# Normed rows turned into columns by the DMA crossbar instead of TensorE, with norm factors folded into weights and a new piece order, in a two-layer graph kernel

## The chip, the cores and the metric

The kernel runs on one core of one Trainium2 chip. The time is the device time of one execution in microseconds (us); the kernel before was run three times. A profile is one separate execution recorded by the hardware profiler; its span runs from the first to the last instruction.

The engines are named as in the profile: PE is TensorE's matmul stream and PEld its weight loads, DVE is VectorE, ACT is ScalarE, POOL is GpSimd, SP is SyncE, which issues most DMAs here. L459 is line 459 of the kernel before.

## The reference, cut to what matters

64 graphs of 256 nodes with 256 features each go through two layers. Every graph is independent of the others; all share the weights.

```python
# layer 0, per graph: x [256,256], adj [256,256] of 0 and 1
h = gat(x, adj, W1, a1); h = gat(h, adj, W2, a2)     # att = softmax(where(adj>0, leaky_relu(e), NEG)); att @ (h W)
h = layernorm(x + h) * g_ln1 + b_ln1                                  # norm A
x = layernorm(h + relu(h @ w_ff1 + b_ff1) @ w_ff2 + b_ff2) * g_ln2 + b_ln2   # norm B
# layer 1: 8 heads of 32
q, k = x @ Wq + bq, x @ Wk + bk
attn = softmax(q k^T / sqrt(32))
out = sum over r in 0..3 of (attn * (adj == r)) @ (x @ Wv[r] + bv[r])
y = layernorm(x + out @ Wo + bo) * g1 + beta1                         # norm C
out = layernorm(y + gelu(y @ W1 + b1) @ W2 + b2) * g2 + beta2         # norm D
```

## The kernel before, in words

**Tiling.** A graph's 256 rows are two tiles of 128 partitions. Everything is fp32. Products with weights want the features on the partitions ("columns"), norms want the nodes there ("rows"), so after norms A, B and C the normed rows are turned into columns: `to_columns` (L355) issues four TensorE transposes of 128x128 into a PSUM bank (L362), and two ACT instructions (L369) copy them out, with the norm's g as scale and its b as bias. The rows are also needed as a residual: `scaled` (L339) multiplies them by g and adds b on POOL (L344, L351). The feed-forward products and the values use seven products in place of eight (`seven_products`, L393), for which `combine` (L378) forms four sums of the columns on POOL (L389).

**Heads.** The scores (L636) go through a maximum on DVE (L643), exponentials on ACT (L650), division by the sums on POOL (L662), and then each of the eight heads' 256x256 weights are turned by the DMA crossbar: `turned` (L272) views the fp32 words as 2-byte halves, lets one DMA transpose turn them (L282, piece `dt`), sorts the halves by four DMAs of 64 KB in pieces of 256 bytes (L290, piece `dm`), and one copy of 128x1024 2-byte values on ACT or POOL joins the halves into fp32 words (L300, piece `mg`). By DVE these are multiplied with the adjacency (L669), and TensorE forms the outputs (L677).

**Order.** The work of a graph is cut into some 170 pieces. Each belongs to one of five stages: L (loads), G (graph attention and norm A), F (feed-forward, norm B, queries and keys), A (attention), T (the rest). The list `PERIOD` (L44) is the order, written out, in which the pieces of one period are issued; in a period graph b is in stage L, graph b-1 in G, b-2 in F, b-3 in A, b-4 in T. The loop at L747 runs 67 periods. Every engine takes its own instructions strictly in this order, so a piece that waits holds up all later pieces of its engine; SP is such a queue too, and carries nearly all DMAs. PSUM has eight banks of one tag "mm", and a matmul piece needs a free one. The tiles of `turned` ("pairs", "halves") have two buffers each.

A piece is named by stage, step and key: `G.gB` is the second graph attention's product (L562), `G.lnA`, `G.rsA`, `G.nmA` are norm A's sums (DVE), root (POOL) and scaling (DVE, L331); `F.ha` to `F.he` are the seven products (L459), `F.hk1` and so on their copies (L438, ACT) and additions (L441, DVE), `F.r0` to `F.r3` the activations (L473, ACT; `T.ge0` to `T.ge3` in layer 1), `F.f0`, `F.f1` the second feed-forward product (L481), `F.q`, `F.k` the queries and keys (L597), `A.sc0`, `A.sc1` scores, `A.va` to `A.ve` values (L610), `A.o0`, `A.o1` outputs (L677), `T.wo` their projection (L696), `T.out` the store.

Weights that are not needed at once are loaded in the first periods (`after`, L257). Ahead of the loop, `joint_weights` (L186) forms W1 W2. After it, a check at L66 to L84 finds whether the adjacency held anything but 0 and 1, in which case a general version would run; here it does not.

Of the kernel before, what the change touches and what calls it, by code (L numbers as in the profile page):

```python
# [25 lines left out]
F32 = mybir.dt.float32  # L26
U8 = mybir.dt.uint8
U16 = mybir.dt.uint16
I32 = mybir.dt.int32
# [4 lines left out]
P = 128  # L34
# [7 lines left out]
STAGES = "LGFAT"  # L42

PERIOD = """  # L44
A.sc0 A.mx02 A.mx00 T.wo A.ex02 G.wh0 A.mx03 A.rz02 A.ex00 A.mx01 A.rz00 T.lnC F.tA A.sp02 G.wc0
F.cA0 F.cA1 A.sp00 A.dt02 A.sc1 A.dt00 G.wh1 A.ex01 F.ha A.mx10 F.sA A.ex03 T.rsC F.hb G.wc1 F.raA
A.ex10 A.mx12 F.hk1 F.hk2 G.eA A.rz01 A.mx13 T.nmC A.dm02 G.lrA T.tC A.ex12 A.rz10 T.cC0 F.hc
A.sp10 G.away A.rz03 T.cC1 F.hp1 A.ex13 A.dm00 A.sp01 A.va G.adA F.hk3 A.mg02 A.rz12 A.vk1 A.dt10
T.ha L.xT A.rz13 A.vb F.hp3 T.hk1 F.hd T.sC T.raC A.mg00 A.vk2 G.exA T.hb A.vc F.hp2 G.rzA A.vp1
T.hk2 F.r0 F.r1 A.mx11 A.vk3 A.dt01 F.he F.hk4 F.rbA F.r2 T.hc G.gA0 A.vd G.gA1 A.dm10 A.vp3 T.hk3  # L50
A.sp03 A.sp13 F.r3 A.mg10 A.ex11 A.dm01 A.dt03 T.hd T.hp3 T.hp2 T.hp1 A.pm02 A.pm10 A.pm00 G.wd0
A.rz11 A.sp11 T.ge0 A.dt13 A.mg01 F.f0 A.vp2 T.ge1 T.he F.f1 T.hk4 G.wd1 T.ge2 T.ge3 T.rbC G.eB
A.sp12 A.pm01 F.lnB G.lrB A.dm03 A.dm13 G.adB A.dt11 A.mg03 F.rsB F.nmB F.raB A.ve T.f0 A.pm03
T.f1 A.mg13 A.dt12 A.dm11 G.exB A.pm13 G.rzB F.tB F.cB0 F.cB1 F.sB G.gB T.lnD A.mg11 A.vk4 G.lnA
A.dm12 L.x F.q T.rsD F.k A.mg12 G.rsA A.o0 F.qe0 F.qe1 A.pm11 A.pm12 T.nmD T.raD F.ke0 T.rbD A.o1
F.ke1 A.oc0 L.adj G.nmA T.out F.rbB A.oc1
# [3 lines left out]
@with_exitstack  # L60
def gnn_stack(ctx: ExitStack, tc: tile.TileContext, t, out: bass.AP):
    nc = tc.nc
    keep = ctx.enter_context(tc.tile_pool(name="keep", bufs=1))

    ends = keep.tile([P, 2, t["x"].shape[0]], F32, name="ends")
    binary(tc, t, ends, out)  # L66
    with ExitStack() as last:
        psum = last.enter_context(
            tc.tile_pool(name="lpsum", bufs=1, space=bass.MemoryType.PSUM)
        )  # L70
        beyond = keep.tile([P, 3], F32, name="beyond")
        nc.vector.memset(beyond, 1.0)
        nc.vector.tensor_scalar(ends[:, 0, :], ends[:, 0, :], 1.0, 1.0, ALU.is_gt, ALU.mult)
        nc.vector.tensor_scalar(ends[:, 1, :], ends[:, 1, :], 0.0, 1.0, ALU.is_lt, ALU.mult)
        nc.vector.tensor_reduce(beyond[:, :2], ends, AX.X, ALU.max)
        total = psum.tile([1, 2], F32, name="total")
        nc.tensor.matmul(total, beyond[:, 2:3], beyond[:, :2], start=True, stop=True)
        found = keep.tile([1, 2], F32, name="found")
        nc.vector.tensor_copy(found, total)
        others = keep.tile([1, 1], I32, name="others")  # L80
        nc.vector.tensor_tensor(others, found[:, 0:1], found[:, 1:2], ALU.max)
    any_other = nc.values_load(others, min_val=0, max_val=P)
    with tc.If(any_other > 0):
        general(tc, t, out)  # L84
# [3 lines left out]
def binary(ctx: ExitStack, tc: tile.TileContext, t, ends, out: bass.AP):  # L88
# [38 lines left out]
    joined = work.tile([P, 4, D], F32, tag="v", name="joined", bufs=1)  # L127
# [17 lines left out]
    def half_factors(name, width, block):  # L145
# [7 lines left out]
        def differences(*before):  # L153
            for to, a, b in (*before, (3, 5, 0), (4, 2, 3), (5, 2, 5), (6, 1, 4)):
                nc.gpsimd.tensor_tensor(f[:, to, :], f[:, a, :], f[:, b, :], ALU.subtract)

        return f, differences

# [5 lines left out]
    def load(do, b):  # L164
# [7 lines left out]
        def adjacency():  # L172
            adj = tiles["adj"] = io.tile([P, NT * N], I32, tag="adj", name=f"adj_{b}", bufs=3)
# [56 lines left out]
    rows = {n: row(t[n], n) for n in ("L0_gnn_g_ln1", "L0_gnn_b_ln1", "L0_gnn_b_ff2")}  # L230
    differences()
    norms.append((column("L0_gnn_g_ln2"), column("L0_gnn_b_ln2")))
    wk, wq = (weight(f"L1_gnn_{n}", KC) for n in ("Wk", "Wq"))
    bk, bq = column("L1_gnn_bk"), column("L1_gnn_bq")
    nc.gpsimd.tensor_scalar(bq, bq, QSCALE, 1.0, ALU.mult, ALU.mult)
# [7 lines left out]
    late = {}  # L243

# [12 lines left out]
    def after(period):  # L257

        if period == 1:
            value_differences((5, 5, 0), (2, 2, 1))  # L260
            late_weights()
            join_biases(("bv1", "bv0", ALU.subtract))
            join_biases(("L0_gnn_b_ln1", "L0_gnn_b_ff2"), ("L0_gnn_b_ln2", "L1_gnn_bo"))
        elif period == 2:
            late["differences"]()
# [6 lines left out]
    def turned(do, stage, key, name, src, tile_of, keep, engine):  # L272
# [5 lines left out]
        def turn():  # L278
            t["pairs"] = work.tile([P, 4, 2, P], U16, tag="pairs", name=f"pairs_{name}", bufs=2)
            words = src()  # L280
            flat = words.rearrange("p a b n -> p (a b n)") if len(words.shape) == 4 else words
            nc.sync.dma_start_transpose(  # L282
                out=t["pairs"].rearrange("p k c q -> p (k c) q"), in_=flat.bitcast(U16)
            )

        def part():
            t["halves"] = work.tile([P, 2, 4, P], U16, tag="halves", name=f"halves_{name}", bufs=2)
            for s in range(2):
                for c in range(2):
                    nc.sync.dma_start(  # L290
                        out=t["halves"][c * 64 : (c + 1) * 64, s, :, :],
                        in_=t["pairs"][s::2, :, c, :],
                    )

        def join():
            to = tile_of()
            keep(to)
            flat = to[:, 0, :]
            copy = nc.scalar.copy if engine == "ACT" else nc.gpsimd.tensor_copy
            copy(  # L300
                flat.bitcast(U16).rearrange("p (n s) -> p s n", s=2),
# [3 lines left out]
        do[f"{stage}.dt{key}"], do[f"{stage}.dm{key}"], do[f"{stage}.mg{key}"] = turn, part, join  # L305


    def layernorm(do, stage, key, name, src):
# [19 lines left out]
        def norm():  # L328
            y = tiles["y"] = work.tile([P, KC, NT, P], F32, tag="y", name=f"y_{name}", bufs=3)
            for i in range(NT):  # L330
                nc.vector.tensor_scalar(  # L331
                    y[:, :, i, :], tiles["acc"][:, i, :].rearrange("p (c d) -> p c d", c=KC),
# [6 lines left out]
    def scaled(do, stage, key, name, tiles, g, b):  # L339


        def times():
            tiles["res"] = work.tile([P, NT, D], F32, tag="res", name=f"res_{name}", bufs=3)
            nc.gpsimd.tensor_tensor(  # L344
                tiles["res"].rearrange("p t (c d) -> p t c d", c=KC),
                tiles["y"].rearrange("p c t d -> p t c d"),
                over_nodes(g).rearrange("p t (c d) -> p t c d", c=KC), ALU.mult,
            )
# [6 lines left out]
    def to_columns(do, stage, key, name, tiles, g, b):  # L355


        def turn():
            ps = tiles["t"] = mm_tile(f"t_{name}")
            for c in range(KC):  # L360
                for i in range(NT):
                    nc.tensor.transpose(  # L362
                        ps[:, c, nodes(i)], tiles["y"][:, c, i, :], ident
                    )

        def scale(c):
            if c == 0:
                tiles["cols"] = work.tile([P, KC, N], F32, tag="cols", name=f"cols_{name}", bufs=3)
            nc.scalar.activation(  # L369
                tiles["cols"][:, c, :], tiles["t"][:, c, :], AF.Identity,  # L370
                bias=b[:, c : c + 1], scale=g[:, c : c + 1],
            )

        do[f"{stage}.t{key}"] = turn
        for c in range(KC):
            do[f"{stage}.c{key}{c}"] = partial(scale, c)
# [116 lines left out]
    def gat(do, b, tiles):  # L493
# [4 lines left out]
        def away():  # L498
# [4 lines left out]
            for at, op in enumerate((ALU.max, ALU.min)):  # L503
                nc.vector.tensor_reduce(ends[:, at, b : b + 1], tiles["adj"], AX.X, op)
# [545 lines left out]
```

## Time and profile before

| What | Value |
|---|---|
| median of 3 runs | 3209.26 us (3208.79 to 3209.77) |
| the profiled execution's own time | 3212.18 us |
| its span | 3210.3 us, mean granted TensorE clock 0.987 |
| ACT busy | 2489.8 us (78%), 6014 instructions |
| DVE busy | 2383.9 us (74%), 5275 instructions |
| POOL busy | 1985.4 us (62%), 2734 instructions |
| DMAs of SP's queue | 342.05 MB in 1172800 packets, 49.4% of the 16 engines' time |
| issue of one DMA transpose on SP | 1245 ns median, 512 times |
| issue of one sorting DMA on SP | 616 ns median, 2048 times |

Busy is the time in which an engine had an instruction in hand. Matmuls overlap, so the times of single matmuls add up to more than the time they take together; what a group of matmuls costs is read from the start of the group to the start of the next. A window of the profile is a stretch of the span, here mostly one period of the order. The chain of work that ended last is followed back from the last instruction; "issue" in it is time in which the engine waited for nothing that the profile shows.

### The profile page before, as it was taken

Reading aid. Unit: us, or ns where it says so; the run is one execution under the profiler, and the core shown is the slowest. Engines: PE = TensorE matmul, PEld = TensorE weight load, DVE = VectorE, ACT = ScalarE, POOL = GpSimd, SP = SyncE. Lnnn points to the kernel's source line nnn. Section 1 sums busy time; section 2 is a strip of 40 time slices with the busy share of each in tenths; the row PEclk is TensorE's granted clock in tenths of the full one; section 3 lists DMA queues with packets and bytes.
Section 4 is the critical chain, followed back from the end, with each engine's and each line's share of the span. In section 5 each row is a group of like instructions: output and inputs, shape, how many; then the busy total and the mean of one; then the engine's idle time right before and its main releaser. Section 6 shows DMA issues by size and latency. Waiting matters only on the chain.

```text
span 3210.3 us, 67241 instructions
## 1 busy us (share of the span) xinstructions
PE 3125.9 (97%) x22410; PEld 2683.9 (84%) x22410; DVE 2383.9 (74%) x5275; ACT 2489.8 (78%) x6014; POOL 1985.4 (62%) x2734
## 2 busy tenths in 40 slices
PE   5899999999999999999999999999999999999996
PEld 3788888888888888888888888888888888888885
DVE  4677777777777777877777877877877777877763
ACT  2678878778778878778778778778778778778773
POOL 4566666656656656656656656656656666666653
PEclk7899999999999999999999999999999999999998
DMA  4455445545445545545445545455545555545542
GB/s 130 97 108 115 107 107 116 108 106 118 107 107 117 108 107 117 107 107 117 107 108 116 107 108 116 107 108 114 108 109 113 109 109 112 110 108 110 109 93 60
DMA packets 1174414, 348.65 MB, mean 109 GB/s; under 512 B 1102736, under 2 KB 1172368, under 8 KB 1174064
## 3 DMA queue, kind: packets, MB, share of 16 engines
q1 hardware_dynamic: 1172800, 342.05, 49.4%
q8 instruction: 181, 2.97, 0.4%
q0 software_dynamic: 976, 1.72, 0.4%
q14 instruction: 169, 1.38, 0.2%
q10 hardware_dynamic: 288, 0.52, 0.1%
HBM read 58.87 MB, written 16.78 MB: 24 GB/s over the span
## 4 chain that ended last, share of the span: by engine, by line
PE 93%; issue 2%; POOL 1%; DMA 1%; SPq 1%; ACT 1%; DVE 1%; POOLq 0%; ACTq 0%; DVEq 0%
PE ff_a L481 13%; PE ff_c L481 13%; PE o L677 7%; PE hX_a L459 7%; PE hX_c L459 7%; PE sc L636 4%; PE wh L509 4%; PE wo L696 4%; PE vX L610 4%; PE hY_a L459 3%; PE gat_b L562 3%; PE hY_c L459 3%; PE gat_a L562 3%; PE q L597 3%; PE k L597 3%
## 5 line engine op out<-in xcount | busy, mean ns | idle before, releaser
L300 ACT COPY pm<-halves_p 128x1024 uint16<-128x1024 uint16 x384 | 514.3, 1355 | 54.0 <-DMA halves_p<-pairs_p 53.1
L481 PE MATMUL ff_a<-w_L_gnn_w_ff,hid_a 128*128 128x256 f32 x2048 | 463.0, 379 | 0.0
L481 PE MATMUL ff_c<-w_L_gnn_W,hid_c 128*128 128x256 f32 x2048 | 456.8, 381 | 2.8 <-ACT hid_c L473 2.8
L481 PEld LDWEIGHTS ff_c<-w_L_gnn_W,hid_c 128*128 128x128 f32 x2048 | 391.8, 191 | 57.7 <-ACT hid_c L473 3.6
L481 PEld LDWEIGHTS ff_a<-w_L_gnn_w_ff,hid_a 128*128 128x128 f32 x2048 | 379.5, 190 | 46.7 <-ACT hid_a L473 0.2
L669 DVE TENSOR_TENSOR pm<-pm,adj 128x512 f32<-128x512 f32 x512 | 345.4, 712 | 25.3 <-ACT pm L300 22.3
L300 POOL COPY pm<-halves_p 128x1024 uint16<-128x1024 uint16 x128 | 171.4, 1339 | 107.7 <-DMA halves_p<-pairs_p 89.6
L677 PE MATMUL o<-pm,v 128*32 128x256 f32 x4096 | 235.1, 381 | 2.7 <-ACT v L438 2.1
L473 ACT ACTIVATE hid_c<-hid_c,col_L_gnn_b 128x256 f32<-128x256 f32 x512 | 224.6, 502 | 3.0 <-DVE hid_c L441 2.0
L473 ACT ACTIVATE hid_a<-hid_a,col_L_gnn_b_ff 128x256 f32<-128x256 f32 x512 | 225.0, 501 | 2.1
L315 DVE TENSOR_TENSOR acc_b<-ff_a,res_a 128x512 f32<-128x512 f32 x64 | 44.2, 691 | 228.8 <-PE ff_a L481 219.5
L677 PEld LDWEIGHTS o<-pm,v 128*32 128x32 f32 x4096 | 126.5, 110 | 101.6 <-POOL rstd_a L326 20.2
L344 POOL TENSOR_TENSOR res_b<-y_b,row_L_gnn_g_ln 128x512 f32<-128x512 f32 x64 | 137.5, 2149 | 106.4 <-DVE y_b L331 106.4
L326 POOL TENSOR_TENSOR rstd_b<-var_b,neghalf 128x2 f32<-128x2 f32 x64 | 67.9, 1061 | 218.4 <-DVE var_b L322 218.4
L688 ACT ACTIVATE oT<-o,col_bv 128x256 f32<-128x256 f32 x128 | 60.7, 474 | 142.1 <-PE o L677 142.1
L636 PE MATMUL sc<-kT,qT 32*128 32x256 f32 x2048 | 154.0, 400 | 1.7 <-ACT p L650 1.2
L509 PE MATMUL wh<-wx,xT 128*128 128x260 f32 x512 | 143.7, 405 | 9.6 <-DVE wx L220 9.6
L438 ACT COPY hid_c<-hX_c 128x512 f32<-128x512 f32 x192 | 116.0, 604 | 43.4 <-PE hX_c L459 43.4
L459 PEld LDWEIGHTS hX_c<-cols_c,f_L_gnn_W 128*128 128x128 f32 x1024 | 135.9, 194 | 9.6 <-DVE hid_c L441 1.9
L459 PEld LDWEIGHTS hX_a<-cols_a,f_L_gnn_w_ff 128*128 128x128 f32 x1024 | 135.9, 194 | 9.2 <-DVE hid_a L441 1.7
L562 PE MATMUL gat_a<-whz_A,s_A 128*128 128x258 f32 x512 | 134.4, 385 | 5.5 <-DVE whz_A L556 5.0
L459 PE MATMUL hX_c<-cols_c,f_L_gnn_W 128*128 128x128 f32 x1024 | 137.0, 277 | 2.2 <-DVE hid_c L441 1.6
(2732 smaller groups left out, 9008.8 us busy)
## 6 DMA issues: line engine op xcount, KB each, us to landing
halves_p<-pairs_p SPq DMA_DIRECT2D x2048, 64.0 KB, 2.1
xT<-in_xT SPq DMA_DIRECT2D x64, 256.0 KB, 3.1
adj<-in_adjT SPq DMA_DIRECT2D x64, 256.0 KB, 2.6
x<-in_x SPq DMA_DIRECT2D x64, 256.0 KB, 2.7
out<-res_d SPq DMA_DIRECT2D x64, 256.0 KB, 2.1
pairs_p<-p SPq DMA_TRANSPOSE x512, 2.8
f_L_gnn_w_ff<-in_L_gnn_w_ff SPq DMA_DIRECT2D x4, 256.0 KB, 9.6
w_L_gnn_w_ff<-in_L_gnn_w_ff SPq DMA_DIRECT2D x1, 1024.0 KB, 11.6
```

The costliest lines, as they stand in the source:

```text
L300: copy(flat.bitcast(U16).rearrange("p (n s) -> p s n", s=2), t["halves"].rearrange("p s k q -> p s (k q)"),)
L344: nc.gpsimd.tensor_tensor(tiles["res"].rearrange("p t (c d) -> p t c d", c=KC), tiles["y"].rearrange("p c t d -> p t c d"), over_nodes(g). ...
L459: nc.tensor.matmul(ps[:, f * P : (f + 1) * P], weights()[0][:, factor, f * P : (f + 1) * P], left, start=start and f == 0, stop=f == FC // ...
L473: nc.scalar.activation(tiles["hid"][:, f, :], tiles["hid"][:, f, :], func, bias=b1[:, f : f + 1])
L481: nc.tensor.matmul(tiles["ff"][:, i, :], tiles["hid"][:, f, nodes(i)], weights()[2][:, f, :], start=(f == 0), stop=(f == FC - 1),)
L509: nc.tensor.matmul(t["whp", j], tiles["xT"][:, c, nodes(j)], wx[:, c, :], start=(c == 0), stop=(c == KC - 1),)
L562: nc.tensor.matmul(ps, t["s"][:, j, nodes(i)], t["whz"][:, j, :width], start=(j == 0), stop=(j == NT - 1),)
L597: nc.tensor.matmul(t[key + "p"][:, o, :], w[:, c, nodes(o)], tiles["cols"][:, c, :], start=(c == 0), stop=(c == KC - 1),)
L610: nc.tensor.matmul(ps, left, wv[:, factor, :], start=start, stop=True, skip_group_check=True)
L636: nc.tensor.matmul(t["sc", g, hh][:, i, :], qkv["q"][hd, g, nodes(i)], qkv["k"][hd, g, :], start=True, stop=True,)
L669: nc.vector.tensor_tensor(pm[:, 1, :], pm[:, 0, :], tiles["adj"], ALU.mult)
L677: nc.tensor.matmul(ps[hh * DH : (hh + 1) * DH, :], qkv["v"][:, j, d0 : d0 + DH], t["pm", (g, hh)][:, r, j * N : (j + 1) * N], start=(r == ...
```

## The change

It does six things.

1. The normed rows of A, B and C are turned into columns by `turned`, as the heads are, with the joining copy on ACT (pieces `F.cA`, `F.cB`, `T.cC`); the TensorE transposes and the two ACT copies are gone, and so is a PSUM bank for each.
2. As that copy cannot scale, g and b of norms A, B and C are folded into the weights that read the columns (`fold_ff`, `fold_values`, `column_bias`, `scale_rows`), once, ahead of the loop or in its first periods.
3. The 2-byte halves are sorted by two DMAs of 128 KB in pieces of 1 KB instead of four. For this the normed rows and the exponentials are written in runs of 64 words, and POOL's product with g becomes two instructions instead of one.
4. The adjacency's check is one maximum over unsigned words instead of a maximum and a minimum.
5. Every piece carries its own lag ("A.sc1/2" is graph b-2's), so that a stage may straddle periods. The lags run from 0 to 5, and the loop has 69 periods. The order is written anew. The two halves of the heads' outputs, `A.o0` and `A.o1`, are no longer neighbours.
6. The adjacency has four buffers instead of three.

```diff
 PERIOD = """
-A.sc0 A.mx02 A.mx00 T.wo A.ex02 G.wh0 ... F.rbB A.oc1
+A.dt10/3 F.hk3/2 A.pm01/4 T.hd/5 A.ex13/3 A.mg13/4 A.dm12/3 A.pm02/4 F.hd/2 A.sc0/3 F.hp3/2
+F.hp2/2 G.lrB/1 L.xT/0 A.o0/4 A.dm10/3 A.pm13/4 L.adj/0 A.mx03/3 F.r0/2 F.r1/2 A.sp11/3 G.adB/1
+A.oc0/4 A.ex03/3 F.he/2 A.rz03/3 A.o1/4 F.hk4/2 A.oc1/4 F.r2/2 F.r3/2 A.sp03/3 A.dt11/3 T.hp2/5
+A.va/3 T.wo/4 A.mx00/3 A.mx01/3 G.exB/1 F.f0/2 A.mg12/3 F.f1/2 A.ex00/3 A.vk1/3 A.mx02/3 T.lnC/4
...
+A.vk2/3 T.dmC/4 T.ge2/5 F.rsB/2 A.vc/3 F.nmB/2 F.dtB/2 A.rz13/3 A.sp13/3 G.wh1/0 T.ge3/5 T.rbC/5
+G.lnA/1 A.mg11/3 G.wc0/0 A.vk3/3 T.f0/5 A.dt01/3 F.dmB/2 G.wc1/0 A.rz00/3 T.cC/4 A.vp1/3 A.ex02/3
+A.sp00/3 A.pm03/3 A.vd/3 A.pm12/3 A.dm01/3 G.eA/0 G.rsA/1 T.f1/5 G.lrA/0 A.vp3/3 G.nmA/1 A.pm11/3
+F.dtA/1 A.dt00/3 F.cB/2 G.adA/0 T.ha/4 A.mg01/3 F.k/2 T.hk1/4 A.rz02/3 F.raB/3 G.exA/0 T.lnD/5
...
 """.split()
...
+    def scale_rows(w, norm):
+        for c in range(KC):
+            for part in w(c):
+                nc.vector.tensor_scalar_mul(part, part, norm[0][:, c : c + 1])
+    def column_bias(bias, norm, block, n):
+        ps = mm_tile("fold", (P, n))
+        for i in range(n):
+            for c in range(KC):
+                nc.tensor.matmul(
+                    ps[:, i : i + 1], block(c, i), norm[1][:, c : c + 1],
...
+        nc.vector.tensor_tensor(bias, bias, ps, ALU.add)
...
+    fold_ff(w1, ff0[1], norms[0])
     differences()
...
         if period == 1:
-            value_differences((5, 5, 0), (2, 2, 1))
+            fold_values()
             late_weights()
...
         elif period == 2:
+            fold_ff(*late["ff1"][:2], norms[2])
             late["differences"]()
...
         def turn():
-            t["pairs"] = work.tile([P, 4, 2, P], U16, tag="pairs", name=f"pairs_{name}", bufs=2)
+            t["pairs"] = work.tile([P, 2, 4, P], U16, tag="pairs", name=f"pairs_{name}", bufs=2)
...
         def part():
-            for s in range(2):
-                for c in range(2):
-                    nc.sync.dma_start(
-                        out=t["halves"][c * 64 : (c + 1) * 64, s, :, :],
-                        in_=t["pairs"][s::2, :, c, :],
-                    )
+            for c in range(2):
+                nc.sync.dma_start(
+                    out=t["halves"][c * 64 : (c + 1) * 64].rearrange("p s k q -> p s (k q)"),
+                    in_=t["pairs"][:, c].rearrange("p k q -> p (k q)"),
+                )
...
         def times():
-            nc.gpsimd.tensor_tensor(
-                tiles["res"].rearrange("p t (c d) -> p t c d", c=KC),
...
+            for i in range(NT):
+                nc.gpsimd.tensor_tensor(
+                    tiles["res"][:, i, :].rearrange("p (k c d) -> p c k d", k=KC, c=2),
...
-    def to_columns(do, stage, key, name, tiles, g, b):
-        def turn():
-            ps = tiles["t"] = mm_tile(f"t_{name}")
-            for c in range(KC):
-                for i in range(NT):
-                    nc.tensor.transpose(
-                        ps[:, c, nodes(i)], tiles["y"][:, c, i, :], ident
-                    )
-        def scale(c):
-            nc.scalar.activation(
-                tiles["cols"][:, c, :], tiles["t"][:, c, :], AF.Identity,
-                bias=b[:, c : c + 1], scale=g[:, c : c + 1],
-            )
+    def to_columns(do, stage, key, name, tiles, engine):
+        def into():
+            tiles["cols"] = work.tile([P, KC, N], F32, tag="cols", name=f"cols_{name}", bufs=3)
+            return tiles["cols"].rearrange("p k n -> p (k n)")
+        do[f"{stage}.c{key}"] = turned(
+            do, stage, key, f"y_{name}", lambda: tiles["y"], into, engine
+        )
...
-            for at, op in enumerate((ALU.max, ALU.min)):
-                nc.vector.tensor_reduce(ends[:, at, b : b + 1], tiles["adj"], AX.X, op)
+            nc.vector.tensor_reduce(most[:, b : b + 1], tiles["adj"].bitcast(U32), AX.X, ALU.max)
...
-        for period in range(1, B + len(STAGES) - 1):
+        for period in range(B + max(lag for _, lag in order)):
...
-            for entry in PERIOD:
-                b = period - STAGES.index(entry[0])
-                if b in graphs:
-                    graphs[b].pop(entry)()
+            for piece, lag in order:
+                if do := graphs.get(period - lag, {}).pop(piece, None):
+                    do()
```

## The prediction

> **What bounds the kernel now.** I read the busy shares first, then windows of one period each, then PE's timeline in one period, then the chain of work at the end. The page's head:
>
> ```profile
> span 3210.3 us, 67241 instructions
> PE 3125.9 (97%) x22410; PEld 2683.9 (84%) x22410; DVE 2383.9 (74%) x5275; ACT 2489.8 (78%) x6014; POOL 1985.4 (62%) x2734
> PEclk7899999999999999999999999999999999999998
> ```
>
> PE is busy to 97%, but a busy PE may be a slow or a waiting one, so I cut the span into periods (columns: length, then busy us and instructions of PE, PEld, DVE, ACT, POOL; granted clock; DMA share; GB/s):
>
> ```profile
> 121.85:170.10 48.25, 44.14 (x318) 37.31 (x318) 31.34 (x64) 36.22 (x93) 25.11 (x38) 0.90 0.47 106
> 170.10:218.35 48.25, 48.23 (x351) 41.58 (x351) 37.01 (x83) 38.91 (x96) 30.63 (x42) 1.00 0.52 109
> 1520.99:1569.24 48.25, 48.23 (x352) 41.59 (x351) 36.86 (x83) 38.83 (x96) 30.62 (x42) 1.00 0.49 110
> 3161.40:3210.30 48.90, 28.15 (x177) 21.64 (x175) 11.42 (x31) 10.35 (x19) 11.37 (x13) 0.82 0.09 23
> ```
>
> From 170 us to about 3065 us a period takes 48.25 us at full clock and PE is never idle. 64 graphs x 48.25 = 3088; the rest, 3210.3 - 3088 = 122 us, is filling and draining the order, partly at a lower clock. ACT has 9.4 us of idle in a period, DVE 11.4, POOL 17.6: these wait for PE, and PE waits for nobody. So a period gets shorter by what PE no longer does, if the rest can follow.
>
> PE's timeline in that period, cut to the transposes and what follows them:
>
> ```profile
> 1527.74 0.60 PE L362 MATMUL t_y<-ident,y_b 128*128 128x128 f32 x4
> 1528.18 1.89 PE L562 MATMUL gat_b<-whz_B,s_B 128*128 128x256 f32 x8
> ...
> 1540.83 0.60 PE L362 MATMUL t_a<-ident,y_a 128*128 128x128 f32 x4
> 1541.36 1.22 PE L636 MATMUL sc<-kT,qT 32*128 32x256 f32 x16
> ...
> 1546.17 0.38 PE L525 MATMUL e_A<-ident,wh_A 128*128 128x128 f32 x2
> 1546.58 0.78 PE L362 MATMUL t_c<-ident,y_c 128*128 128x128 f32 x4
> 1547.19 1.06 PE L459 MATMUL hX_a<-S_a,f_L_gnn_w_ff 128*128 128x128 f32 x8
> ```
>
> Durations overlap, so I go from start to start: t_y 0.44, t_a 0.53, t_c 0.61 us. Ahead of t_c, e_A takes 0.41 where its twin e_B takes 0.22 (1568.43 to 1568.65): 0.19 more spent waiting for y_c. That is 1.77 us of a period.
>
> **The change, part by part.**
>
> *Transposes off PE.* -1.77 us x 64 = -113 us, all of it on the path, since PE is the path in 60 of the periods. If the 0.19 reappears at another edge: -101.
>
> *More changes of tile shape on PE.* The two outputs, 64 matmuls into 32-column tiles, ran in one piece; now scores, `o0`, `he`, `o1`, `va` alternate. Such an edge shows 0.1 us over the plain rate: `F.k`, with the outputs behind it, takes 1.82 us from start to start, and `T.wo` behind the scores 1.83, where `F.q`, as many matmuls of the same shape, takes 1.72. Two more edges: +0.1 to +0.2, I take +0.12. The period becomes 48.25 - 1.77 + 0.12 = 46.6 us, the saving 64 x 1.65 = 106.
>
> *The turn itself.* A head's turn at the end of the chain, where nothing else runs, shows every step:
>
> ```profile
> 3157.74 2.74 DMA pairs_p<-p
> 3160.56 0.60 SPq L290
> ...
> 3165.20 2.11 DMA halves_p<-pairs_p
> 3167.41 1.35 ACT pm L300
> ```
>
> 2.74 transpose, two sorting issues instead of four (2 x 0.64), 2.11 landing, 1.35 copy: 7.5 us. By TensorE a turn took 1.15 + 1.03 = 2.2 us in the same drain (t_c, then the two L369). So each norm's columns come 5.3 us later. Inside the saturated stretch this is cover against PE's list in the new order. From the end of `F.f1` to the start of `F.k` PE has 15.0 us of other work (`he`, values, `gB`, `wh`, `f0`, `f1`, `T.ha`, each at its row's start-to-start time); the chain is sums 2.1, root 1.06, scaling 0.73 to 1.7, turn 7.5: 11.4 to 12.4. From `G.gB` to `F.ha` 19.7 us against 12 plus the queues; from `T.wo` to `T.ha` 20. I cost the turns at 0 there. If the cover is gone, each us late costs 64 us, and the next to be late is `F.q`, then the scores.
>
> Here a rule speaks against the change. The Trainium skill, "VectorE: DVE Perf Modes", The three transpose paths and Rules for kernel authors, says to transpose 128x128 by TensorE if a PSUM destination is fine, else by the crossbar, with 390 against 1309 ns for a 2-byte block. By that price eight blocks a turn would be 10.5 us, and 11 turns a period 115 us of DMA: an order bound by DMAs at over 7000 us. The row says 2.74 us for a turn's eight blocks, and SP issues the next after 1.25 us. I follow the row: the rule compares a block's latency, while here PE's time is the scarce thing and DMA is half idle.
>
> *ACT.* Six L369 (30.8 us in ten periods) leave: -3.08; three copies of 1.36 arrive: +4.07. 38.8 + 1.0 = 39.8 of 46.6 us, 85%. The exponentials written in runs of 64 words have no row; nearest is the same ACTIVATE at 470 ns to runs of 128. I take 0; [...]a tenth more on each of 16 would be +0.75 us a period. Both hide in ACT's remaining 6.8 us.
>
> *POOL.* The product with g becomes two halves. The sums' rows (128x128 in 0.456, 128x512 in 1.27 us) give 0.18 fixed + 2.1 ns a column, so +0.18 x 4 = 0.7: 31.3 of 46.6. *DVE.* One reduce less (0.63): 36.2. The unsigned maximum and norms written in runs of 64 I take at their present rows.
>
> *PSUM and buffers.* Three banks fewer are asked for in a period and a fourth adjacency buffer is there: no row shows a wait for either, so 0, and a gain is excluded while PE never idles.
>
> *SP and DMA.* Issues per period: 8 x 1.245 + 32 x 0.616 + loads 1.6 = 31.3 us now; 11 x 1.245 + 22 x 0.616 + 1.6 = 28.9 then. Each new pair of turns is queued in front of head turns, and heads behind it wait up to one issue and a landing (3 us), which the 1.3 us saved per head and SP's own idle, 17 us of a period, cover. DMA share: two transposes alone show 0.64 of the engines over 2.85 us, so 0.9 engine-us each; three more are 2.7, and pieces of 1 KB for 256 bytes take no more than now. 23.8 + 2.7 of 46.6 us: at most 57%.
>
> *Fill and drain.* 122 us now. Added: the fold stands in front of the first graph (`wh` at 21.65 us will wait for Wq, issued at 14.35 and 7.8 to land, then eight small matmuls, and DVE scales w_ff1 between the steps that make wx): +3, ends 0 and +8. For the first and the last graph the turns are bare, at most 3 x 5.3 at each end, partly under other graphs' work: +17, ends 0 and +32. Taken away: sorting issues of eight heads in the drain, where they stand in the chain (1.3 each): -8, ends -10 and 0. The sixth lag spreads the fill over more, emptier periods; by the same PE work and no new chain I take 0, ends -20 and +20. Sum +12: 134 us, ends about 95 and 170.
>
> *Sum* against the profiled execution: 64 x 46.6 + 134 = 3116 us of span. The median of the runs lies 1.0 us under that span: 3115.
>
> **The rivals.**
>
> *ACT's waits stay (chance 0.2).* ACT idles 9.4 us of a period now, in waits for PE, with 1.0 us more to do. Its wait for t_y (1.4 us) goes; if the other 8 stay and none overlaps, a period is 39.8 + 8 = 47.8; halfway, 47.3, the time is 64 x 47.3 + 134 = 3160. For it: four score banks, held until ACT's exponentials empty them, stand between `sc1` and `gA0`, some 4.5 us with three exponentials of 0.91 behind one turned copy. Against it: most of ACT's waits are slack for pieces whose consumer comes later.
>
> *A turned norm misses its slot, slower (0.05).* The place is `F.k`: the copy of norm B's turn stands on ACT behind a copy for norm C's, an exponential and `lrA`, which itself waits for PE's `e_A`, and its sorting on SP behind another transpose. The price is (chain - 15.0) x 64; it eats the whole gain from a chain of 16.8 us. At 18 it would be 3115 + 192 = 3307. Against it: the measured steps sum to 12.4, and what stands in front on SP and ACT adds about 3.
>
> *It does less than it says (0.08).* PE gets shorter, but the emptier first and last periods take a good part back: 200 us of fill and drain, 66 over the forecast's, give 3181. For it: five incomplete periods at each end where there were three. Against it: they hold the same work, and the present drain was bound by sorting issues that are halved.
>
> *Better than forecast (0.15)*: no new edges and ends of 100 us: 64 x 46.48 + 100 - 1 = 3074.
>
> **How the numbers follow.** The forecast, a period of 46.4 to 46.8 and a fill and drain of 110 to 150, has 0.5: 3080 to 3145. Faster than that 0.15, ACT 0.2, fill 0.08, late turn 0.05, within 0.2% by some mix 0.02. A measurement of this kernel can tell 0.2%, 6 us. The range from 3072 to 3168 leaves out the late turn, the worst fill and the far ends. Faster 0.93, same 0.02, slower 0.05.
>
> **What will show it.** A steady period near 46.6 us with PE busy throughout proves the first term; PE's row must have no L362 group, and the edges around `o0` show the second. Idle of PE ahead of `k`, `ha` or `ff` released by ACT's copy of a turn is the late turn; PE's wait for a bank that an exponential frees is ACT's rival. The first full period's start (126 us now) and the time from the last full period to the end (about 138 us) show fill and drain. I am wrong if the period stays above 47.2, or if the ends exceed 170 us together.

## The result and the profile after

The changed kernel takes 3156.55 us (median of 4 runs, 3154.80 to 3158.29) against 3209.52 us of the kernel before beside it (4 runs, 3208.79 to 3211.23): 0.9834 of the time, with a 95% interval from 0.9817 to 0.9851. It is 53 us faster; 94 had been forecast. The profiled execution's own time is 3158.29 us.

The head of the page after (span; busy us, share and count of each engine; granted clock in 40 slices):

```profile
span 3156.4 us, 64811 instructions
PE 3048.8 (97%) x21734; PEld 2613.1 (83%) x21734; DVE 2459.1 (78%) x5231; ACT 2555.5 (81%) x5822; POOL 2122.4 (67%) x2990
PEclk8899999999999999999999999999999999999998
```

PE is still the engine that is busy all the time. As before, the page's averages hide where the time went, so the span has to be cut. I cut it at the start of each graph's first `k` product, which comes once in a period. Windows of the changed kernel (length, then busy us and instructions of PE, PEld, DVE, ACT, POOL; granted clock; DMA share; GB/s): the time to the first graph's `k`, two neighbouring periods, and the time from the last graph's `k` to the end:

```profile
0.00:105.48 105.48, 56.51 (x223) 47.44 (x223) 43.66 (x98) 21.86 (x52) 32.78 (x52) 0.82 0.45 116
1511.86:1559.65 47.79, 47.05 (x340) 40.41 (x339) 38.15 (x82) 40.71 (x92) 32.82 (x47) 1.00 0.69 149
1559.65:1606.30 46.65, 46.65 (x340) 40.20 (x339) 38.06 (x82) 40.48 (x93) 32.81 (x47) 1.00 0.78 149
3058.51:3156.40 97.89, 66.26 (x458) 52.28 (x458) 38.81 (x87) 46.84 (x93) 42.57 (x59) 0.88 0.39 81
```

The same cuts of the kernel before:

```profile
0.00:85.38 85.38, 45.31 (x168) 35.47 (x169) 34.89 (x74) 19.36 (x49) 35.52 (x55) 0.78 0.46 122
3120.92:3210.30 89.38, 59.29 (x385) 46.09 (x383) 30.29 (x73) 36.21 (x80) 31.98 (x44) 0.83 0.24 58
```

Read them as a sum: the periods, the start and the end. An undisturbed period takes 46.65 us where it took 48.25, with PE busy throughout: over the 63 intervals between 64 graphs that is 100.8 us. Before, all steady periods were alike; now 21 of 58 are more than 0.1 us longer than 46.65, up to 48.54, so that those 58 lose 13.2 us together (the few periods at either end that are not full lose another 5.1 against before). The first `k` stands 20.1 us later, and the stretch after the last is 8.5 us longer. 100.8 - 13.2 - 5.1 - 20.1 - 8.5 = 53.9 us, the difference of the two spans.

PE's timeline in the undisturbed period shows what the saving is made of (start, duration):

```profile
1573.70 0.38 PE L560 MATMUL e_B<-ident,wh_B 128*128 128x128 f32 x2
1573.92 1.06 PE L495 MATMUL hX_c<-S_c,f_L_gnn_W 128*128 128x128 f32 x8
1574.81 1.06 PE L495 MATMUL hX_a<-S_a,f_L_gnn_w_ff 128*128 128x128 f32 x8
...
1576.87 1.93 PE L721 MATMUL o<-pm,v 128*32 128x256 f32 x32
1578.74 1.16 PE L495 MATMUL hX_a<-cols_a,f_L_gnn_w_ff 128*128 128x128 f32 x8
1579.83 1.93 PE L721 MATMUL o<-pm,v 128*32 128x256 f32 x32
1581.69 0.70 PE L645 MATMUL vX<-f_Wv,cols_y 128*128 128x256 f32 x2
...
1600.84 0.38 PE L560 MATMUL e_A<-ident,wh_A 128*128 128x128 f32 x2
1601.06 3.62 PE L517 MATMUL ff_c<-w_L_gnn_W,hid_c 128*128 128x256 f32 x16
```

There is no transposing group left. `e_A` takes 0.22 us from start to start like `e_B`; its 0.19 of waiting is gone. The outputs in two halves take 1.87 + 1.86 = 3.73 us where they took 3.60, and `hX_a` between them 1.09 where such a piece elsewhere takes 0.89 (1573.92 to 1574.81): a change of shape costs about a tenth, as costed. What the edges add in all, by difference, is 1.77 - 1.60 = 0.17 us a period.

### The profile page after: what moved, and what is told of

Same layout as the page of the kernel before. It is cut to its first block, busy times and chain, and to the rows that moved or that the text cites. A ratio compares the mean times of both kernels' runs of the same rounds, so it can differ in the third digit from the quotient of the medians.

```text
span 3156.4 us, 64811 instructions
## 1 busy us (share of the span) xinstructions
PE 3048.8 (97%) x21734; PEld 2613.1 (83%) x21734; DVE 2459.1 (78%) x5231; ACT 2555.5 (81%) x5822; POOL 2122.4 (67%) x2990
## 4 chain that ended last, share of the span: by engine, by line
PE 85%; DMA 5%; ACT 3%; DVE 3%; POOL 2%; issue 2%; SPq 0%; ACTq 0%; POOLq 0%; DVEq 0%
PE ff_a L517 13%; PE ff_c L517 12%; PE o L721 7%; PE hX_a L495 7%; PE hX_c L495 6%; PE sc L671 4%; PE vX L645 3%; PE k L632 3%; PE wo L740 3%; PE wh L544 3%; PE q L632 3%; PE gat_b L597 3%; PE hY_c L495 3%; PE gat_a L597 3%; PE hY_a L495 3%; DMA halves_p<-pairs_p 3%
## 5 line engine op out<-in xcount | busy, mean ns | idle before, releaser
L713 DVE TENSOR_TENSOR pm<-pm,adj 128x512 f32<-128x512 f32 x512 | 465.4, 926 | 87.4 <-POOL pm L345 63.6
L721 PE MATMUL o<-pm,v 128*32 128x256 f32 x4096 | 249.9, 383 | 1.3 <-ACT pm L345 0.9
L721 PEld LDWEIGHTS o<-pm,v 128*32 128x32 f32 x4096 | 120.7, 110 | 98.5 <-issue 16.7
L425 POOL TENSOR_TENSOR S_a<-cols_a 128x128 f32<-128x128 f32 x128 | 58.5, 457 | 179.2 <-ACT cols_a L345 179.2
L495 PE MATMUL hX_a<-cols_a,f_L_gnn_w_ff 128*128 128x128 f32 x1024 | 144.6, 285 | 13.3 <-ACT cols_a L345 9.2
L495 PE MATMUL hX_a<-S_a,f_L_gnn_w_ff 128*128 128x128 f32 x1024 | 138.2, 278 | 9.1 <-ACT hid_a L474 9.0
L345 ACT COPY cols_y<-halves_y_y 128x1024 uint16<-128x1024 uint16 x64 | 86.5, 1352 | 74.5 <-DMA halves_y_y<-pairs_y_y 74.4
L632 PE MATMUL k<-cols_y,w_L_gnn_Wk 128*128 128x256 f32 x512 | 127.2, 393 | 18.5 <-ACT cols_y L345 18.5
L495 PE MATMUL hX_c<-S_c,f_L_gnn_W 128*128 128x128 f32 x1024 | 141.7, 281 | 2.2 <-ACT hid_c L474 2.2
L495 PEld LDWEIGHTS hX_a<-S_a,f_L_gnn_w_ff 128*128 128x128 f32 x1024 | 130.0, 192 | 16.7 <-ACT hid_a L474 12.6
L495 PEld LDWEIGHTS hX_c<-S_c,f_L_gnn_W 128*128 128x128 f32 x1024 | 124.2, 191 | 23.0 <-issue 19.6
```

The lines of the kernel that those rows point to most:

```text
L345: copy(into().bitcast(U16).rearrange("p (n s) -> p s n", s=2), t["halves"].rearrange("p s k q -> p s (k q)"),)
L495: nc.tensor.matmul(ps[:, f * P : (f + 1) * P], weights()[0][:, factor, f * P : (f + 1) * P], left, start=start and f == 0, stop=f == FC // ...
L632: nc.tensor.matmul(t[key + "p"][:, o, :], w[:, c, nodes(o)], tiles["cols"][:, c, :], start=(c == 0), stop=(c == KC - 1),)
L713: nc.vector.tensor_tensor(pm[:, 1, :], pm[:, 0, :], tiles["adj"], ALU.mult)
L721: nc.tensor.matmul(ps[hh * DH : (hh + 1) * DH, :], qkv["v"][:, j, d0 : d0 + DH], t["pm", (g, hh)][:, r, j * N : (j + 1) * N], start=(r == ...
```

## The experiments

All were timed five times (the second one seven times) beside the kernel before, which took 3210.63 to 3212.17 us there. The theory was that the turns are hidden in an undisturbed period, and that the 41 us missing against the forecast are lost in two other places: at the start, to the fold, and in the uneven periods, to something that the turns do to SP or the DMAs.

**The old order without transposes.** In the kernel before, ACT's two copies read the normed rows themselves; nothing is turned.

```diff
         def turn():
-            ps = tiles["t"] = mm_tile(f"t_{name}")
-            for c in range(KC):
-                for i in range(NT):
-                    nc.tensor.transpose(
-                        ps[:, c, nodes(i)], tiles["y"][:, c, i, :], ident
-                    )
+            pass
...
-                tiles["cols"][:, c, :], tiles["t"][:, c, :], AF.Identity,
+                tiles["cols"][:, c, :], tiles["y"][:, c, :, :].rearrange("p i n -> p (i n)"), AF.Identity,
```

> The kernel before in its own order, with its TensorE transposes left out: the ACT instructions that copied them out of PSUM read the normed rows instead, so the columns are not turned. Theory (PE alone is the path, and a transpose costs what its row shows from start to start): a steady period of 48.25 - 1.77 = 46.5 us, and no more at the ends than before: 3209.5 - 113 = 3096. Rival (another engine or the order is close behind PE): the period stays above 47.2 us with idle time of PE, 3140 or more.

Measured: 3160.91 us, 0.9842 [0.9829, 0.9856]; the period is 47.44 us, not 46.5. The rival was right: only 0.8 of the 1.77 us leave the period. PE's weight loads show one thing that came in their place (waits between 400 and 2900 us: total us, times, longest):

```profile
PEld vZ L605 <- DVE hid_a L436: 46.7, 52, 0.9
```

In 52 periods one of the values' products now waits for a bank that DVE has to empty. PE itself loses about 0.55 us of the missing 0.96 there: from the start of `vX` to that of `vZ` takes 1.09 us, where it took 0.54. The rest lies in pieces that each became some 0.07 to 0.09 us longer. So taking the transposes off PE is not enough: as the old order stands, the next limit is 0.8 us behind. Something else of the change lets the period come down to 46.65, most likely its order; no run put the new order alone beside this one.

**The new order with the transposes on TensorE.** The reverse: everything of the change but the turned norms, which use four TensorE transposes and one copy of ACT.

```diff
+        def turn():
+            ps = tiles["t"] = mm_tile(f"t_{name}")
+            for c in range(KC):
+                for i in range(NT):
+                    nc.tensor.transpose(
+                        ps[:, c, nodes(i)], tiles["y"][:, c, i, :], ident
+                    )
```

> The changed kernel with TensorE transposes for the norms again, at the place of the sorting DMAs in the new order, and one ACT copy out of PSUM; fold, heads' sorting and order stay. Theory (the time comes from the transposes off PE, the new order gives nothing of itself while they are there): a period of 46.65 + 1.3 and an edge or two, 48.0 to 48.3, ends 10 to 20 us shorter than the change's: 3210, within 15. Rival (the order is the gain): a period of 47.2 or less, 3165.

Measured: 3200.68 us, 0.9970 [0.9958, 0.9981]; every steady period takes 47.97 us. Its timeline of PE:

```profile
1516.89 0.60 PE L414 MATMUL t_c<-ident,y_c 128*128 128x128 f32 x4
1517.33 0.60 PE L655 MATMUL vX<-f_Wv,S_y 128*128 128x256 f32 x2
...
1522.53 0.60 PE L414 MATMUL t_y<-ident,y_b 128*128 128x128 f32 x4
1522.96 0.60 PE L655 MATMUL vX<-f_Wv,S_y 128*128 128x256 f32 x2
...
1530.58 0.60 PE L414 MATMUL t_a<-ident,y_a 128*128 128x128 f32 x4
1531.02 1.89 PE L642 MATMUL q<-cols_y,w_L_gnn_Wq 128*128 128x256 f32 x8
```

0.44 us each from start to start, 1.31 a period: that is 47.97 - 46.65 to a hundredth. The theory held in the main: the turned norms are worth 1.32 us a period. That the rest "gives nothing of itself" was nearly so: new order and new sorting together give 0.28.

**The fold left out.** The weights stay as loaded; g and b of norms A, B and C are not applied in the columns.

```diff
-        for c in range(KC):
-            for part in w(c):
-                nc.vector.tensor_scalar_mul(part, part, norm[0][:, c : c + 1])
+        return
...
-        ps = mm_tile("fold", (P, n))
...
-        nc.vector.tensor_tensor(bias, bias, ps, ALU.add)
+        return
```

> The changed kernel without the fold of g and b into the weights (the factors of norms A, B and C are left out of the columns). Theory (the fold stands in the way of the first graph: its 46 matmul records run from 20.6 to 30.6 us just ahead of the first graph's product, and two later folds hold up the first products again): the first keys and queries come some 13 to 18 us earlier, steady periods as they are, 3140. Rival (the turns' latency fills the ends, the fold lies beside it): at most 3 us, 3153.

Measured: 3137.91 us, 0.9772 [0.9758, 0.9785]. That is 18.6 us less than the changed kernel. The first `k` stands at 90.33 us instead of 105.48, and 19 of 58 steady periods are still uneven. So the fold costs 15.2 us ahead of the first `k` and has nothing to do with the uneven periods. The chain of waits of the changed kernel shows both places of it (start, duration):

```profile
7.45 13.13 DMA f_L_gnn_w_ff<-in_L_gnn_w_ff
20.62 9.98 PE fold L173 x46
30.60 3.64 PE wh L544 x8
...
57.03 3.19 DMA pairs_y_a<-y_a
...
60.92 3.03 DMA halves_y_a<-pairs_y_a
63.98 1.34 ACT cols_a L345
...
75.02 0.79 PE fold L173 x8
75.80 0.98 PE fold L286 x4
77.17 1.59 DVE f_Wv L166 x4
...
79.95 1.21 DVE hid_a L477 x2
```

The first block is 24 products with a single column each. The profile has two records of each; 46 of these 48 stand here and take 9.98 us, 0.22 a record. `wh`, which started at 21.65 us before, starts at 30.60. The second block, for the values, stands in front of DVE's `hid_a` of the first graph.

**The fold made later.** The same products and scales, hung on pieces of the first four periods where PE waits for the first graphs; w_ff1's columns are summed in the gaps at `G.eA` and `G.eB`.

```diff
-    fold_ff(w1, ff0[1], norms[0])
-    differences()
...
+    hooks = {
+        (0, "G.eA"): first_sums, (0, "G.eB"): more_sums, (1, "G.rzB"): first_scales,
+        (1, "G.rsA"): first_differences, (1, "G.eA"): query_sums, (1, "G.nmA"): query_scales,
+        (2, "F.dtB"): fold_values, (3, "F.dtB"): late_fold,
+    }
```

> The changed kernel with the fold's pieces put where PE and DVE wait anyway: the first weights' sums behind the first graph's products, the queries' behind the second's, the values' and the last ones' while the second and third feed-forward block's norm is turned. Theory (the 18.6 us that the kernel without fold gained are its place, not its work): 12 to 18 us less than the change, 3141. Rival (the sums' PE time itself is what costs): 3152 or more.

Measured: 3141.08 us, 0.9786 [0.9773, 0.9800], first `k` at 91.89 us. That is 3.2 us more than without the fold: its work is nearly free where PE idles; it was its place that cost.

**The norms not turned.** ACT's copy reads the normed rows in place of the sorted halves; no DMA for them. The heads are turned as in the change.

```diff
+        def straight():
+            nc.scalar.copy(
+                into().bitcast(U16).rearrange("p (n s) -> p s n", s=2),
+                tiles["y"].rearrange("p c a b n -> p (c a b n)").bitcast(U16)
+                .rearrange("p (n s) -> p s n", s=2),
+            )
```

> The changed kernel with norms A, B and C not turned: the joining copy on ACT reads the normed rows themselves, so their transpose and their two sorting DMAs are gone and the columns are wrong; heads, fold and order stay. Theory (the turns' latency and the load that they put on the DMA engines make the irregular periods, mean 46.9 against a floor of 46.65, and a part of the ends): all periods at 46.65, -15 us, and some 6 us less for each turn that stands bare at the ends, five of them, -30: 3111. Rival (order and fold make the ends): periods even out, the ends stay, 3141. Second rival (the irregular periods come from ACT or from the banks, not from DMAs): 3150 or more, periods as uneven as they are.

Measured: 3120.27 us, 0.9717 [0.9704, 0.9730]. All steady periods take 46.65 us; the first `k` is 9.2 us earlier than in the changed kernel, the stretch after the last 6.9 us shorter, and the five periods at either end that are not full take 11.7 us less together. Two things follow: nothing of the turns is in the undisturbed period, and at the ends the turns cost 9.2 + 6.9 + 11.7 = 27.8 us, as too little other work hides them there.

**The heads not turned.** The opposite half: the three norms go through SP and the DMAs, the eight heads do not (with a sixth buffer for the exponentials).

> The changed kernel with the heads not turned (their joining copy reads the weights themselves, one more buffer for these; the attention's outputs are wrong), norms turned as in the change. DMAs fall by 8 of 11 turns. Theory (the irregular periods come from turns that queue behind one another on SP and on the DMA engines, 70% busy): the norms' turns land in about 2.7 and 2.1 us, all periods at 46.65 and the heads' part of the ends goes: 3120. Rival (the norms' own latency is what is late, whatever else runs): periods as uneven as now, 3140 to 3150.

Measured: 3130.96 us, 0.9748 [0.9735, 0.9762], all steady periods 46.65. The periods are as the theory said; the time is 11 us above its 3120. Uneven periods need both kinds of turns, not the norms' turns as such.

**Three buffers.** Between "too much for the DMAs" and "too few tiles" this decides, as it moves the same bytes by the same instructions.

```diff
-            t["pairs"] = work.tile([P, 2, 4, P], U16, tag="pairs", name=f"pairs_{name}", bufs=2)
+            t["pairs"] = work.tile([P, 2, 4, P], U16, tag="pairs", name=f"pairs_{name}", bufs=3)
...
-            t["halves"] = work.tile([P, 2, 4, P], U16, tag="halves", name=f"halves_{name}", bufs=2)
+            t["halves"] = work.tile([P, 2, 4, P], U16, tag="halves", name=f"halves_{name}", bufs=3)
```

> The changed kernel with three buffers instead of two for the turned pairs and for the sorted halves. Theory A (the irregular periods come from SP, which waits for a buffer that the turn before last still holds, and holds up the turns behind it): periods even at 46.65, 12 to 15 us less, 3142. Theory B (the turns are late because the 16 DMA engines are busy to 70% in bursts): periods as uneven as now, 3153 or more.

Measured: 3139.81 us, 0.9780 [0.9767, 0.9793]. All 58 steady periods take 46.65 us, with the DMA queue at 69.6% of the engines' time against 70.0% in the changed kernel. It was the buffers. SP's waits between 400 and 2900 us in the changed kernel:

```profile
SPq L330 <- DMA halves_p<-pairs_p: 186.4, 201, 1.7
SPq L338 <- DMA pairs_p<-p: 165.0, 232, 2.5
SPq L330 <- POOL p L698: 129.6, 107, 2.1
...
SPq L330 <- DMA halves_y_a<-pairs_y_a: 76.9, 53, 2.5
```

and with three buffers, from the top of the list:

```profile
SPq L330 <- POOL res_d L399: 269.7, 53, 5.9
SPq L338 <- DMA pairs_p<-p: 156.5, 183, 2.5
```

The first line of the changed kernel is SP, about to issue a transpose, waiting for a sorting DMA to have read the tile that the transpose will write; the last is the same for norm A's turn. With three tiles no such wait is among the chief ones, and SP waits mostly for what POOL delivers; as all periods are even, that costs PE nothing. How 1 us gets from SP to PE is seen by laying ACT's timeline of the long period (from 1511.86) over that of the undisturbed one (from 1559.65):

```profile
1526.22 1.34 ACT L345 COPY pm<-halves_p 128x1024 uint16<-128x1024 uint16 x1 [1.39 <-DMA halves_p<-pairs_p]
1527.43 0.57 ACT L474 COPY hid_a<-hX_a 128x512 f32<-128x512 f32 x1
...
1572.39 1.36 ACT L345 COPY pm<-halves_p 128x1024 uint16<-128x1024 uint16 x1
1573.60 0.59 ACT L474 COPY hid_a<-hX_a 128x512 f32<-128x512 f32 x1
```

with SP's (the second line of each pair holds the sorting DMAs of two heads, that of the copy's among them):

```profile
1518.33 2.63 SPq L330 DMA_TRANSPOSE pairs_p<-p  x2
1521.58 3.11 SPq L338 DMA_DIRECT2D halves_p<-pairs_p  x4
...
1564.50 2.65 SPq L330 DMA_TRANSPOSE pairs_p<-p  x2
1567.81 2.86 SPq L338 DMA_DIRECT2D halves_p<-pairs_p  x4
```

and PE's line in the long one:

```profile
1528.06 1.16 PE L495 MATMUL hX_a<-S_a,f_L_gnn_w_ff 128*128 128x128 f32 x8 [0.74 <-ACT hid_a L474]
```

Counted from each period's `k`: the pair of transposes goes out after 6.47 us against 4.85, ACT's copy starts after 14.36 against 12.74, the copy of `hid_a` queued behind it after 15.57 against 13.95, and `hX_a`, which needs the bank that this copy frees, after 16.20 against 15.16. A turn that is 1.6 us late costs PE 1.0 us, through an ACT instruction that has nothing to do with the turn but stands behind it. The wait for the buffer is there too: in both periods this pair of transposes goes out 0.07 to 0.08 us after norm A's sorting, two turns earlier, has landed (1518.25 and 1564.43). That turn itself already was 2.0 us late in the long period.

This is one period. In about 14 of the 21 long ones the largest loss is at this same `hX_a`; the other seven lose less at any one place and were not traced. As idle time of PE the wait shows only a part of the 13.2 us; how the rest of the lateness reaches PE stays open:

```profile
PE hX_a L495 <- ACT hid_a L474: 4.9, 10, 1.4
```

**Four sorting DMAs a turn.** The changed kernel with the heads' and norms' halves sorted as before, in four DMAs of 64 KB and pieces of 256 bytes.

```diff
-            for c in range(2):
-                nc.sync.dma_start(
...
+            for s in range(2):
+                for c in range(2):
+                    nc.sync.dma_start(
+                        out=t["halves"][c * 64 : (c + 1) * 64, s, :, :],
+                        in_=t["pairs"][s::2, :, c, :],
+                    )
```

> The changed kernel with the sorting as before: four DMAs of 64 KB in pieces of 256 bytes per turn, runs of 128 words, for heads and norms. Theory (the larger pieces save no DMA time, 2.96 against 2.86 us of the 16 engines per turn, but SP's issues: 11 x 1.25 + 44 x 0.62 + 1.6 = 42.6 us of a period of 46.65 leave SP no room for its waits): SP's queue runs late every period, periods of 47.5 to 49, 3200 to 3290. Rival (SP has room enough; a sort's landing of 2.1 instead of 3.1 us makes up for two more issues): 3150 to 3165.

Measured: 3623.30 us, 1.1277 [1.1261, 1.1292]. Right in kind, and 3.5 to 11 times as large as expected: the steady periods take 52 to 56 us. SP's timeline shows nearly one issue after the other, while the DMAs are less busy than in the changed kernel (61.5%):

```profile
1500.87 2.57 SPq L339 DMA_DIRECT2D halves_y_c<-pairs_y_c  x4
1503.48 1.33 SPq L330 DMA_TRANSPOSE pairs_y_y<-y_b  x1
1505.28 1.23 SPq L330 DMA_TRANSPOSE pairs_p<-p  x1
1506.71 2.58 SPq L339 DMA_DIRECT2D halves_y_y<-pairs_y_y  x4
```

Eleven turns at 1.245 + 4 x 0.64 us are 41.9, with the loads 43.5 us of a period of 46.65: on paper it fits. But SP takes its list strictly in order, and each sorting waits for its own transpose, which lands 3.2 us after issue in the median; with so little slack those waits seem no longer to fit between the issues. In this order and with two buffers, turned norms pay only with the halved sorting; four sorting DMAs with three buffers were not run.

**Late fold and three buffers.** Both edits that gained, in one kernel.

> The changed kernel with both single edits that gained: the fold's products and scales moved into the graphs' gaps, and three buffers for pairs and halves in place of two. Theory: they mend different losses, the fold one of the start and the buffers one of the steady periods, so the gains add: 15.5 us and 16.7 us off 3156.6 give 3124; the first k product stands near 92 us, and every steady period is 46.65 us. Rival: the two share time (with the start's turns already eased by the third buffer, the late fold only moves its work onto periods that then lengthen), and the time is 3135 us or more.

Measured: 3127.79 us (3126.73 to 3130.37), 0.9738 [0.9725, 0.9751], with the first `k` at 92.47 us and all 58 steady periods at 46.65. The gains add but for 4 us; the late fold leaves two early periods of 47.55 and 49.42 us. This kernel beats the changed one by 0.9%, and is the fastest here that leaves nothing out.

## Why the prediction was right in direction and too large

*Transposes off PE, edges, the period.* Forecast 46.6, measured 46.65; the edges 0.12, measured 0.17. Of these 1.60 us the experiments give 1.32 to the transposes and 0.28 to the order and the heads' sorting. The prediction booked the whole 1.77 to the transposes; the 0.19 before `t_c` and what edges they made belonged to the place of the pieces. The same removal in the old order brought 0.8 us: that the rest "can follow" was a condition, and the changed kernel meets it.

*The turn at no cost.* The bare turn was put at 7.5 us; at the start it takes 8.3 (57.03 to 65.32). In an undisturbed period it costs PE nothing, as said: without the norms' turns the period is the same. The rival of a late turn before `F.k` did not come about; PE's waits for that copy are 0.2 us in all between 400 and 2900 us. The Trainium skill's rule that was weighed ("VectorE: DVE Perf Modes", Rules for kernel authors), TensorE where a PSUM destination is fine, would have kept the kernel at 3200.68 us; the trace was the better guide.

*PSUM and buffers: the step that failed for the periods.* It says that no row shows a wait for either, and takes 0 for both. It thought of PSUM and of the adjacency. The tiles of `turned` with their two buffers were not costed, though the change gives them three more users a period and makes each hold its tile longer: the sorting lands after 3.3 us where it took 2.1. SP's waits for these tiles cost 13.2 us in the steady periods, and 16.7 us in all by the third buffer.

*DMA.* "At most 57%", from three more transposes of 0.9 engine-us each; measured 70.0%. The norms' sorting was forgotten. From the two kernels with a part of the turns, 52.5% of 3115.5 us with 512 turns and 22.0% of 3129.4 us with 192, a turn with its sorting takes 2.96 engine-us: three are 8.9, not 2.7. It did no harm: with three buffers 69.6% go with even periods.

*Fill and drain: the term that was mis-sized.* By the forecast's own measure, span less 64 periods, it was 122 us; 134 were forecast, and 3156.4 - 64 x 46.65 = 171 measured. The sign that was set for being wrong, ends above 170 us, thus came up, if only just. By the same measure the new order with the transposes on TensorE has 3198.9 - 64 x 47.97 = 129 us, the kernel with the norms not turned 130, and three buffers 153. So the 49 us by which 171 exceeds 122 can be split, as an estimate:

- Uneven steady periods, put at 0: 13.2.
- The bare turns, +17 within 0 and 32: 171 - 129 - 13.2 = 29, of which the third buffer takes back about 5. The term is low, but inside its ends.
- The fold, +3 within 0 and 8: 15.2 in front of the first `k`. This is the step that failed. The working let `wh` wait for Wq and "eight small matmuls", but PE takes all 24, w_ff1's 16 first, before `wh`, and the values' fold stands in front of the first graph's `hid_a` too.
- The sorting issues, -8, and the new order, 0: the kernel with TensorE transposes, which has the fold, is 7 us above the kernel before, so these two together gave some 9 back. No run tells them apart. The halved issues save 1.3 us a head, and by the medians the sorting then lands 1.2 us later, which speaks for the order.

*ACT, POOL, DVE.* ACT +1.0 us a graph, measured (2555.5 - 2489.8) / 64 = 1.0. POOL +0.7, measured 2.1; DVE -0.6, measured +1.2, of which its product with the adjacency alone is 8 x (926 - 712 ns) = 1.7. All of it lies beside PE. What goes with DVE's longer product stands in the last section; POOL was not followed up.

*The rivals.* "ACT's waits stay" gave 3160 us, near the measured time, but by a longer period everywhere, and the undisturbed period denies it. Something of it was real: ACT's queue carries a late turn to PE. Its waits for turns in the 2500 us, 24.5 us for heads before, became 88.2 for heads and 52.0 for norm B. "It does less than it says" named the place of part of the loss; its cause, emptier periods, was not it: with TensorE transposes the same order has ends of 129 us.

*Luck.* 3156.55 lies outside 3080 to 3145, which had half the chance, and inside the range to 3168 because that range also took in ACT's waits (3160). What filled it were other losses: the fold's place, the two buffers and the turns at the ends.

## What to carry to other kernels

When work moves from the limiting engine to a queue, cost what it asks of that queue: issues, the time each buffer is held, and the instructions that stand behind the piece which now waits. One more buffer for each tile can be the difference between hidden and nearly hidden: here it is worth 17 us of 3157. One-time work "ahead of the loop" is not free when it stands in front of the first product; put it where the first iterations leave the engine idle.

## What was not expected of the hardware

- Larger pieces did not spare the DMA engines: sorting in pieces of 1 KB takes (70.0% x 3156.4 - 120) / 704 = 2.97 engine-us a turn with its transpose, in pieces of 256 bytes (61.5% x 3624.0 - 120) / 704 = 3.00 (120 engine-us for the rest, from the two kernels with fewer turns). What they spare is SP: two issues of 0.6 us each a turn.
- A matmul with a single column is not cheap, and its time goes with its weight load. The 46 records of the first fold take 0.22 us each, with weight loads of 333 ns; most of the 32 records of the last fold take 0.11 us, with loads of 192 ns. The granted clock of the first fold's stretch reads 1.00, but the clock's own records begin only at 34.03 us in this trace. The last fold settles it: its loads change from 192 to 333 ns where the record falls to half, at 122.8 us, as the loads of other products do at the other changes of the record up to 201 us:

```profile
119.72:122.63 2.91, 2.91 (x29) 2.91 (x28) 0.00 (x0) 1.33 (x6) 0.00 (x0) 1.00 0.65 152
122.96:123.60 0.64, 0.64 (x4) 0.64 (x5) 0.00 (x0) 0.00 (x0) 0.00 (x0) 0.50 0.79 263
```

  So the first fold ran at the pace of half the clock, and a 1.00 ahead of the first record says nothing; the 0.82 of the window to the first `k` is too high for the same reason. At the later pace its 46 records would have taken about 46 x 0.11 = 5 us (an estimate) instead of 9.98.
- DVE's product with the adjacency rose from 712 to 926 ns in the changed kernel, and is 886 to 927 in the others of the new order. The runs of 64 words are not the cause, as it is 886 with four sorting DMAs and runs of 128; nor is the traffic of the turns (924 with the heads not turned). It depends on what POOL does beside it. With POOL idle it takes 688 ns on average in the changed kernel (60 times) and 684 before (198 times); next to POOL's addition L399 1470 (66 times), next to its product L392 1171 (62 times). One such place:

```profile
1572.15 1.28 POOL L399 TENSOR_TENSOR res_d<-res_d,row_L_gnn_beta 128x512 f32<-128x512 f32 x1
1572.45 1.52 DVE L713 TENSOR_TENSOR pm<-pm,adj 128x512 f32<-128x512 f32 x1
```

  The new order puts more of these side by side; no run moved them apart.
